# Cross-attention on one core: score tiles from products of 234, 234 and 156 columns in place of 308 and twice 154

## The chip, the core and the metric

The kernel runs on one NeuronCore of a Trainium2 chip. The core has five engines with a queue of instructions each: PE (TensorE, matrix products; its weight loads are listed as PEld), DVE (VectorE), ACT (ScalarE), POOL (GpSimd) and SP (SyncE, which here only issues DMAs). Each engine works through its own queue strictly in the order written; they meet through semaphores. Products go to PSUM, everything else lies in SBUF or in DRAM. The metric is the device time of one execution in microseconds (us); lower is better.

## The reference, cut to what matters

The input x holds 32 batches of 512 queries with 640 channels, and the context 32 batches of 77 keys with 1024 channels. Text, object, other and IP keys are named in the reference, but with 77 context rows only the text part has any keys, so this is left:

```python
q = heads(x @ to_q_w)                      # 20 heads of 32 channels
k, v = heads(ctx @ to_k_w), heads(ctx @ to_v_w)
s = einsum('bhqd,bhkd->bhqk', q, k) / sqrt(32)
p = softmax(s, axis=-1)                    # over 77 keys
out = merge(einsum('bhqk,bhkd->bhqd', p, v)) @ to_out_w + to_out_b + x
```

All of it is float32. The kernel reaches that with products of a faster format (fp32r) by splitting each operand a into a high part (the rounded value) and a low part (the rest), and adding three products: high by high, low by high, high by low.

## The kernel before, in words

A *chunk* is 128 channels of one batch, which is four heads of 32; a batch has five chunks and the kernel 160. Keys and values of all batches are made at the start and stored in DRAM (`k_dram`, `v_dram`). Then a loop runs over the batches. For each chunk it does the following, with the names of the functions and tiles:

- `queries` (L542): 15 products of 512 columns put the chunk's queries into the PSUM tile `pq`. ACT writes their high part to `qt[:, 0]` (`high_query`, L779). POOL copies halves of it to other rows (`copy_query`, L783), and DVE writes the low parts beside them (`low_query`, L787, two instructions). Tile `qt` has three planes of 128 rows: plane 0 the high queries of all four heads; plane 1 the low queries of heads 0 and 1 in rows 0 to 63 and a copy of their high queries in rows 64 to 127; plane 2 the same for heads 2 and 3.
- `score_tile` (L577): for each of four groups of 128 queries, three products into one PSUM tile `sc` of four heads by 77 keys: plane 0 by the high keys of all heads (308 columns), plane 1 and plane 2 by high and low keys of two heads each (154 columns). The weights of these products, which PE must load first, are 128 by 128 pieces of `qt`; the moving operand is the key tile `kb`.
- `load_head_keys` (L512): the key tiles `kb` (`kb0` for chunks 0 to 2 of a batch, `kb1` for chunks 3 and 4) are refilled for every batch by DMAs from `k_dram` on SP's queue, two for each of four heads and each of the two tiles: 16 in a batch. The high keys are needed twice, and the second copy is made by POOL (`copy_half_keys`, L519, four in a batch).
- `score_max` (L588, DVE), `exps` (L602, ACT: four exponentials with their sums), `sums` (L612, DVE), `normalize` (L617, POOL, over the whole chunk's `pn`), `block_transpose` (L624, DVE), then out to DRAM and back in another layout (`store_p` L633, `load_rows` L648 and L650).
- `cast_rows` (L661, L663, ACT), `rest_p` (L672, DVE) and `last_p` (L679, POOL) split the probabilities into high and low parts `pp`; `value_pass` (L694) makes six products of 512 columns from them, into `pa`.
- `lower_half`, `add_halves`, `high_a`, `low_a` (L708, L712, L726, L731) sum and split the result, and `project` (L750) multiplies by `to_out_w`: 24 products of 320 columns to a chunk. The residual and the bias come in through `xr` (`add_bias`, L743, POOL; `add_output`, L765, DVE).
- The next batch's x is transposed by DVE (L306) and split by ACT (L316) and POOL (`low_x`, L320).

The order of all this is written out by hand in three lists of tokens: FILL for batches 0 and 1 and the start, PLAN for each of the batches 2 to 30, LAST for the rest. A token such as `3k0` is an operation (`k`: one `copy_query`) of the chunk 3 places on from the batch's first; `s` is a score tile, `l` is `last_p`, `R` is `rest_p`, `N` the normalization, `uk` a load of keys. `run` walks a list and each token appends its instructions to the queues of its engines. So each engine's order is that of its tokens in the list.

Of the kernel before, what the change touches and what calls it, by code (L numbers as in the profile page):

```python
# [8 lines left out]
F32 = mybir.dt.float32  # L9
FPR = mybir.dt.float32r  # L10
AF = mybir.ActivationFunctionType
ALU = mybir.AluOpType
# [19 lines left out]
NBLK = HPC * KPAD // Q  # L32

# [18 lines left out]
def kernel(  # L52
# [394 lines left out]
    def open_small():  # L447
        nonlocal small
        if small is None:
            kvc.release()  # L450
            xpool.append(ctx.enter_context(tc.tile_pool(name="xparts", bufs=1, reuse_waits="tile")))
            small = ctx.enter_context(tc.tile_pool(name="small", bufs=1, reuse_waits="tile"))
            kbs.append(small.tile([P, 4, GROUPS[0][1], KCOLS // 2], FPR, name="kb0"))
# [9 lines left out]
    def open_second():  # L463
        nonlocal z
        if not vbs:
# [3 lines left out]
            kbs.append(pool.tile([P, 4, GROUPS[1][1], KCOLS // 2], FPR, name="kb1"))  # L469
# [33 lines left out]
    def load_keys(b, g, heads=range(HPC), parts=(0, 1)):  # L503
        j0, nj = GROUPS[g]
        src = k_dram[g][:, :, :, b * NKEY : (b + 1) * NKEY].bitcast(F32)
        kb = kbs[g].bitcast(F32)
        for i in heads:
            own, half = slice(i * HD, (i + 1) * HD), slice(i % 2 * NKEY, (i % 2 + 1) * NKEY)
            other = slice(*((i + 2) % HPC * HD + k for k in (0, HD)))
            for part, rows in enumerate((own, other)):  # L510
                if part in parts:
                    nc.sync.dma_start(kb[rows, 1 + i // 2, :, half], src[own, part])  # L512

    def load_head_keys(b, g, i, part):
        load_keys(b, g, (i,), (part,))

    def copy_half_keys(g, h):
        kb, rows = kbs[g], slice(64 * h, 64 * h + 64)
        nc.gpsimd.tensor_copy(kb[rows, 3 * h], kb[rows, 1 + h].bitcast(F32))  # L519

    def copy_keys(g):
        copy_half_keys(g, 0)
        copy_half_keys(g, 1)
# [26 lines left out]
    def split_q(n):  # L550

        qt, pq = qts[n % 2], pqs.pop(n)
        nc.scalar.copy(qt[:, 0, :], pq)
        lower, upper = slice(0, 64), slice(64, P)
        halves = ((lower, upper), (upper, lower))
        for w, (r, other) in enumerate(halves):
            nc.gpsimd.tensor_copy(qt[other, 1 + w, :], qt[r, 0, :].bitcast(F32))
        for w, (r, other) in enumerate(halves):
            nc.vector.tensor_tensor(
                qt[r, 1 + w, :], pq[r], qt[r, 0, :].bitcast(F32), ALU.subtract  # L560
            )

    def score_tile(n, t):
        b, j = divmod(n, NC_)
        g = GROUP_OF[j]
        qt, kb = qts[n % 2], kbs[g]
        jg = j - GROUPS[g][0]
        sc = ps.tile([P, S], F32, tag="sc", name="sc", bufs=3)
        half = KCOLS // 2
        for m, (cols, keys_) in enumerate(  # L570
            (
                (slice(0, KCOLS), kb[:, 0::3, jg]),
                (slice(0, half), kb[:, 1, jg]),
                (slice(half, KCOLS), kb[:, 2, jg]),
            )
        ):
            nc.tensor.matmul(  # L577
                sc[:, cols],
                qt[:, m, t * P : (t + 1) * P],
                keys_,  # L580
                start=(m == 0),
                stop=(m == 2),
            )
        return sc

    def score_max(sc):
        nm = small.tile([P, HPC], F32, tag="nm", name="nm", bufs=3)
        nc.vector.tensor_reduce(  # L588
            nm, sc[:, :KCOLS].rearrange("p (h k) -> p h k", k=NKEY), AX.X, ALU.max, negate=True
        )  # L590
        return nm

    def scores(n, t):
        sc = score_tile(n, t)
        return sc, score_max(sc)

    def exps(n, t, sc, nm):
        if n not in sms:
            sms[n] = small.tile([P, NQ * HPC], F32, tag="sm", name="sm", bufs=2)
        for i in range(HPC):  # L600
            at = t * HPC + i
            nc.scalar.activation(  # L602
                pnb[n % 2][:, at, :NKEY],
                sc[:, i * NKEY : (i + 1) * NKEY],
# [176 lines left out]
    def copy_query(n, w):  # L781
        qt, half = qts[n % 2], (slice(0, 64), slice(64, P))
        nc.gpsimd.tensor_copy(qt[half[1 - w], 1 + w, :], qt[half[w], 0, :].bitcast(F32))  # L783

    def low_query(n, w):
# [342 lines left out]
```

## Time and profile before

| | |
|---|---|
| time, median of 3 runs | 1860.13 us (1859.85 to 1861.66) |
| span of the profiled execution, first to last instruction | 1856.5 us |
| time of the runs that lies around that span (the profiled execution's own time is not given apart) | 3.4 to 5.2 us, 3.6 at the median |
| granted PE clock | 1.000 |
| matrix products | 10332 |
| POOL instructions | 1120 |
| DMA: mean rate over the span | 232 GB/s |
| HBM read and written | 247 MB and 182 MB |

A busy share adds the recorded times of an engine's instructions. Products are recorded longer than the distance at which they follow each other, so a PE of 99% busy may still wait a little. The program has a start of some 250 us (keys and values), a filling stretch of two batches, and then repeats itself from batch to batch until close to the end; a batch has 5 x (15 + 12 + 6 + 24) = 285 products.

### The profile page before, as it was taken

What the parts mean: (1) busy time and instruction counts of PE and PEld (TensorE: products, weight loads), DVE (VectorE), ACT (ScalarE), POOL (GpSimd) and SP (SyncE); (2) the same over time, 40 slices, a digit from 0 to 9 for tenths busy, and PEclk for the clock granted to TensorE, in tenths of its full rate; (3) what the DMA queues carried; (4) which work ended last, traced back from release to release, by engine and by line L of the source; (5) the groups of instructions that cost most, each with busy time, mean ns of one, the idle gap of its engine ahead of it and who ended that gap; (6) DMA issues with size and microseconds to landing.
All of it is one profiled execution on the core that took longest, in us unless ns stands there. A gap on an engine that the chain in (4) does not pass through costs nothing.

```text
span 1856.5 us, 37492 instructions
## 1 busy us (share of the span) xinstructions
PE 1842.4 (99%) x10332; PEld 1655.7 (89%) x10332; DVE 1563.4 (84%) x2502; ACT 1527.2 (82%) x6218; POOL 1303.9 (70%) x1120
## 2 busy tenths in 40 slices
PE   9999999999999999999999999999999999999998
PEld 7888897889999999999999999999999999999998
DVE  5445458899999999999999999999999999999996
ACT  3233248899999999999999999999999999999984
POOL 1100268778788788778778877887778878877874
PEclk9999999999999999999999999999999999999999
DMA  9889779998998898888998888998889988888875
GB/s 188 199 198 249 184 193 256 254 242 235 247 240 243 240 238 232 242 235 236 238 244 237 234 243 237 244 238 237 235 234 244 244 241 236 237 232 243 228 228 187
DMA packets 563296, 431.37 MB, mean 232 GB/s; under 512 B 191120, under 2 KB 471120, under 8 KB 563088
## 3 DMA queue, kind: packets, MB, share of 16 engines
q1 hardware_dynamic: 558192, 413.16, 84.5%
q0 software_dynamic: 4800, 15.65, 2.7%
q8 instruction: 85, 1.39, 0.3%
q14 instruction: 123, 1.01, 0.2%
q10 hardware_dynamic: 96, 0.16, 0.0%
HBM read 247.17 MB, written 181.64 MB: 231 GB/s over the span
## 4 chain that ended last, share of the span: by engine, by line
PE 93%; DMA 4%; SPq 1%; DVE 1%; ACT 1%; issue 0%; POOL 0%; DVEq 0%; ACTq 0%; POOLq 0%
PE po L750 29%; PE pq L542 28%; PE pa L694 12%; PE sc L577 11%; PE pv L204 7%; PE pk L204 6%; DMA pd<-z 1%; DMA cs<-in_ctx_dram 1%; DMA xr<-in_x_dram 1%; DMA wo_s<-wo_dram 0%; DMA wraw<-in_L_xattn_to_v_w_dram 0%; DMA xs<-in_x_dram 0%; DMA wraw<-in_L_xattn_to_k_w_dram 0%; ACT pn L602 0%; DMA raw<-pd 0%
## 5 line engine op out<-in xcount | busy, mean ns | idle before, releaser
L602 ACT ACTIVATE pn<-sc,nm 128x77 f32<-128x77 f32 x2560 | 797.1, 343 | 36.0 <-DVE nm L588 29.6
L750 PE MATMUL po<-wo_s,at 128*128 128x320 f32 x3840 | 707.2, 310 | 0.1
L750 PEld LDWEIGHTS po<-wo_s,at 128*128 128x128 f32 x3840 | 619.7, 188 | 41.1 <-DVE xr L765 0.6
L542 PE MATMUL pq<-xt,wq_s 128*128 128x512 f32 x2400 | 596.7, 394 | 2.9 <-ACT pp L661 1.9
L602 ACT ACTIVATION_READ_ACCUMULATOR pn<-sc,nm 128x1 f32 x2560 | 567.5, 222 | 0.0
L542 PEld LDWEIGHTS pq<-xt,wq_s 128*128 128x128 f32 x2400 | 436.7, 188 | 82.5 <-ACT pp L661 2.1
L617 POOL TENSOR_TENSOR pn<-pn,rs 128x1232 f32<-128x1232 f32 x160 | 389.4, 2434 | 94.0 <-DVE rs L612 90.0
L694 PE MATMUL pa<-pp,vb 128*128 128x512 f32 x960 | 340.9, 403 | 4.1 <-DVE at L731 3.3
L577 PEld LDWEIGHTS sc<-kb,qt 128*128 128x128 f32 x1920 | 302.9, 188 | 14.4 <-ACT pn L602 1.8
L588 DVE TENSOR_REDUCE nm<-sc 128x4 f32<-128x308 f32 x640 | 295.0, 466 | 21.6 <-PE sc L577 16.7
L577 PE MATMUL sc<-kb,qt 128*128 128x154 f32 (+1 forms) x1920 | 301.9, 274 | 0.9 <-ACT pn L602 0.9
L783 POOL CAST qt<-qt 64x512 fp32r<-64x512 f32 x320 | 196.9, 615 | 139.5 <-ACT qt L779 124.4
L712 DVE TENSOR_TENSOR pa<-pa,aw 64x512 f32<-64x512 f32 x320 | 222.3, 695 | 50.4 <-ACT aw L708 43.2
L679 POOL TENSOR_TENSOR pp<-raw,pp 64x512 fp32r<-64x512 f32 x160 | 207.0, 1294 | 66.9 <-ACT pp L661 53.5
L624 DVE STREAM_TRANSPOSE z<-pn 128x1280 f32<-128x1280 f32 x160 | 241.2, 1507 | 8.8 <-DMA pd<-z 3.4
L708 ACT COPY aw<-pa 64x1024 f32<-64x1024 f32 x160 | 162.2, 1014 | 85.0 <-PE pa L694 83.9
L787 DVE TENSOR_TENSOR qt<-pq,qt 64x512 fp32r<-64x512 f32 x320 | 216.8, 678 | 13.9 <-ACT qt L779 9.0
L320 POOL TENSOR_TENSOR xt<-xs,xt 128x512 fp32r<-128x512 f32 x160 | 204.6, 1305 | 20.8 <-ACT xt L316 15.8
L743 POOL TENSOR_TENSOR xr<-xr,bias 128x640 f32<-128x640 f32 x128 | 202.3, 1581 | 13.1 <-issue 3.5
L672 DVE TENSOR_TENSOR pp<-raw,pp 128x1024 fp32r<-128x1024 f32 x160 | 195.7, 1223 | 0.0
L694 PEld LDWEIGHTS pa<-pp,vb 128*128 128x128 f32 x960 | 173.8, 189 | 15.1 <-DVE pp L672 2.3
L663 ACT CAST pp<-raw 128x1024 fp32r<-128x1024 f32 x160 | 168.1, 1051 | 0.7 <-DMA raw<-pd 0.7
(46 smaller groups left out, 1584.2 us busy)
## 6 DMA issues: line engine op xcount, KB each, us to landing
pd<-z SPq DMA_DIRECT2D x640, 160.0 KB, 3.4
raw<-pd SPq DMA_DIRECT2D x160, 512.0 KB, 4.5
xr<-in_x_dram SPq DMA_DIRECT2D x128, 320.0 KB, 3.9
out_dram<-xr SPq DMA_DIRECT2D x127, 320.0 KB, 3.7
xs<-in_x_dram SPq DMA_DIRECT2D x124, 320.0 KB, 5.8
raw<-pd SPq DMA_DIRECT2D x160, 128.0 KB, 4.2
v_dram<-vs SPq DMA_DIRECT2D x80, 192.0 KB, 4.0
k_dram<-ks POOLq DMA_DIRECT2D x20, 512.0 KB, 4.2
```

The source lines that it names most:

```text
L204: nc.tensor.matmul(held[j][:, :gn], w[:, k, a, :], cts[g, k][:, c, :gn], start=(k == 0 and n == 0), stop=(k == NK - 1 and n == 2),)
L542: nc.tensor.matmul(pqs[n], wq_s[:, k, a, j * P : (j + 1) * P], xts[b, k][:, c, :], start=(k == 0 and m == 0), stop=(k == NC_ - 1 and m == 2),)
L577: nc.tensor.matmul(sc[:, cols], qt[:, m, t * P : (t + 1) * P], keys_, start=(m == 0), stop=(m == 2),)
L588: nc.vector.tensor_reduce(nm, sc[:, :KCOLS].rearrange("p (h k) -> p h k", k=NKEY), AX.X, ALU.max, negate=True)
L602: nc.scalar.activation(pnb[n % 2][:, at, :NKEY], sc[:, i * NKEY : (i + 1) * NKEY], AF.Exp, bias=nm[:, i : i + 1], accum_out=sms[n][:, at : ...
L617: nc.gpsimd.tensor_tensor(pf, pf, rs.unsqueeze(2).to_broadcast([P, NQ * HPC, NKEY]), ALU.mult)
L624: nc.vector.transpose(z.rearrange("p b t j -> p t b j"), pn.rearrange("p (t h) k -> p t (h k)", t=NQ).rearrange("p t (b i) -> p t b i", i=Q),)
L679: nc.gpsimd.tensor_tensor(pp[64:, 4, :], raw[:64, 2, :], pp[:64, 4, :].bitcast(F32), ALU.subtract)
L694: nc.tensor.matmul(pas[n][:, p, :], vb[:, p, t, :], pp[:, c, :], start=(c == p), stop=(c == p + 2),)
L712: nc.vector.tensor_tensor(pa[64 * p : 64 * p + 64, 0], pa[:64, p], aw[:, p], ALU.add)
L750: nc.tensor.matmul(pos[b, t, h][:, :HALF], ats[b * NC_ + j][:, a, t * P : (t + 1) * P], wos[0][:, j, c, h * HALF : (h + 1) * HALF], start= ...
L787: nc.vector.tensor_tensor(qt[rows, 1 + w, :], pqs[n][rows], qt[rows, 0, :].bitcast(F32), ALU.subtract)
```

## The change

It makes the same score tile from other pieces. Three products have 3 x 4 = 12 quadrants of 32 rows to fill, and four heads have three terms each, which is 12 as well. The heads now stand in the tile in the order 2, 0, 1, 3, each in a block of 78 columns of which 77 are used. The first product covers the blocks of heads 2, 0 and 1 (234 columns), the second those of heads 0, 1 and 3 (234), the third those of heads 2 and 3 (156). `KEYS_OF` says into which product, quadrant and block each of a head's three key pieces (high, low, high again) goes; `COPIES` says which quadrants of `qt` hold copies of high queries.

```diff
+KBLK = NKEY + 1
+ORDER = (2, 0, 1, 3)
+KEYS_AT = (0, 3 * KBLK, 6 * KBLK)
+KEYS_OF = (
+    ((0, 0, 1), (0, 3, 1), (1, 0, 0)),
+    ((0, 1, 2), (1, 2, 1), (1, 1, 1)),
+    ((0, 2, 0), (2, 0, 0), (2, 2, 0)),
+    ((1, 3, 2), (2, 1, 1), (2, 3, 1)),
+)
+COPIES = ((2, 0, 64, 64), (1, 96, 96, 32), (1, 64, 32, 32), (0, 96, 0, 32))
...
-    def copy_half_keys(g, h):
-        kb, rows = kbs[g], slice(64 * h, 64 * h + 64)
-        nc.gpsimd.tensor_copy(kb[rows, 3 * h], kb[rows, 1 + h].bitcast(F32))
...
     def load_head_keys(b, g, i, part):
-        load_keys(b, g, (i,), (part,))
+        src = k_dram[g][i * HD : (i + 1) * HD, part % 2, :, b * NKEY : (b + 1) * NKEY].bitcast(F32)
+        m, quad, block = KEYS_OF[i][part]
+        c0 = KEYS_AT[m] + block * KBLK
+        nc.sync.dma_start(
+            kbs[g].bitcast(F32)[quad * HD : (quad + 1) * HD, :, c0 : c0 + NKEY], src
+        )
...
+        for m, heads in enumerate((blocks[:, 0:3], blocks[:, 1:4], blocks[:, 0::3])):
+            nh = (3, 3, 2)[m]
+            keys_ = kb[:, KEYS_AT[m] : KEYS_AT[m] + nh * KBLK].rearrange("p (h k) -> p h k", k=KBLK)
             nc.tensor.matmul(
-                sc[:, cols],
+                heads,
                 qt[:, m, t * P : (t + 1) * P],
                 keys_,
                 start=(m == 0),
                 stop=(m == 2),
+                skip_group_check=True,
             )
...
-        for i in range(HPC):
-            at = t * HPC + i
+        for i, head in enumerate(ORDER):
+            at = t * HPC + head
...
     def copy_query(n, w):
-        qt, half = qts[n % 2], (slice(0, 64), slice(64, P))
-        nc.gpsimd.tensor_copy(qt[half[1 - w], 1 + w, :], qt[half[w], 0, :].bitcast(F32))
+        qt, (m, r1, r0, rn) = qts[n % 2], COPIES[w]
+        nc.gpsimd.tensor_copy(qt[r1 : r1 + rn, m, :], qt[r0 : r0 + rn, 0, :].bitcast(F32))
```

So a chunk now has four `copy_query` instead of two: one of 64 rows and three of 32. The last of them puts the high queries of head 0 over those of head 3 in plane 0, so it must come after the copies that read head 3 there and after the second `low_query`. The four `copy_half_keys` of a batch are gone, and the second high keys come by DMA: 24 key loads in a batch instead of 16. FILL and LAST keep their order but for the new tokens; PLAN is a new list. Line numbers after L500 are smaller by up to 27 in the new kernel (L783 is L759, L617 is L593, L577 is L558).

On POOL's queue, a stretch of about a batch in the repeating part (`qt` are the query copies, `kb` the key copies, `pn` the normalization, `pp` is `last_p`, `xt` is `low_x`, `xr` the bias). Before:

```order
L679 TENSOR_TENSOR pp<-raw,pp 64x512
L617 TENSOR_TENSOR pn_1922<-pn_1922,rs 128x16x77
L783 CAST qt_1920<-qt_1920 64x512 x2
L519 CAST kb_2003<-kb_2003 64x308 x2
L743 TENSOR_TENSOR xr<-xr,bias 128x640
L617 TENSOR_TENSOR pn_1921<-pn_1921,rs 128x16x77
L783 CAST qt_1919<-qt_1919 64x512 x2
L679 TENSOR_TENSOR pp<-raw,pp 64x512
```

And now:

```order
L655 TENSOR_TENSOR pp<-raw,pp 64x512
L593 TENSOR_TENSOR pn_1924<-pn_1924,rs 128x16x77
L759 CAST qt_1922<-qt_1922 32x512
L759 CAST qt_1922<-qt_1922 64x512
L330 TENSOR_TENSOR xt<-xs,xt 128x512
L759 CAST qt_1922<-qt_1922 32x512 x2
L330 TENSOR_TENSOR xt<-xs,xt 128x512 x2
L655 TENSOR_TENSOR pp<-raw,pp 64x512
```

The key copies have gone, each pair of query copies has become four, and they now stand in two groups with other work between them.

On PE's queue, around a score tile (`sc`) with products of `po` (projection) and `pa` (values) beside it. Before:

```order
L577 MATMUL sc<-kb_1753,qt_1919 128x308
L577 MATMUL sc<-kb_1753,qt_1919 128x154 x2
L694 MATMUL pa<-pp,vb_2005 128x512
L750 MATMUL po<-wo_s,at_2690 128x320 x3
L577 MATMUL sc<-kb_1753,qt_1919 128x308
L577 MATMUL sc<-kb_1753,qt_1919 128x154 x2
```

And now:

```order
L558 MATMUL sc<-kb_2007,qt_1923 128x234 x2
L558 MATMUL sc<-kb_2007,qt_1923 128x2x78
L670 MATMUL pa<-pp,vb_2010 128x512 x3
L726 MATMUL po<-wo_s,at_2714 128x320 x6
L558 MATMUL sc<-kb_2007,qt_1923 128x234 x2
L558 MATMUL sc<-kb_2007,qt_1923 128x2x78
```

The tile is still three products, of 624 columns in all instead of 616, and the other products stand around it in another order.

On SP's queue, where the last keys of the next batch's first tile (`kb_1753`) are called for, with the returns of probabilities (`raw`) and x (`xs`) near them. Before:

```order
L512 DMA kb_1753<-k_dram_60 32x3x77
L648 DMA raw<-pd 128x2x512
L633 DMA pd<-z 32x10x128
L512 DMA kb_1753<-k_dram_60 32x3x77
L633 DMA pd<-z 32x10x128 x3
```

And now:

```order
L517 DMA kb_1753<-k_dram_60 32x3x77 x2
L626 DMA raw<-pd 64x512
L517 DMA kb_1753<-k_dram_60 32x3x77
L312 DMA xs<-in_x_dram 32x16x160 x2
L626 DMA raw<-pd 64x512
L517 DMA kb_1753<-k_dram_60 32x3x77
```

There are twelve of these loads where eight stood. In the list the last of them now comes behind the third score tile of the batch's last chunk; before, it came just ahead of that chunk's first.

More of the change, by code (lines that the diff above doesn't have):

```diff
@@ L452, in open_small @@
             small = ctx.enter_context(tc.tile_pool(name="small", bufs=1, reuse_waits="tile"))
-            kbs.append(small.tile([P, 4, GROUPS[0][1], KCOLS // 2], FPR, name="kb0"))
+            kbs.append(small.tile([P, GROUPS[0][1], 8 * KBLK], FPR, name="kb0"))
     def open_first():
@@ L468, in open_second @@
             pool = ctx.enter_context(tc.tile_pool(name="second", bufs=1, reuse_waits="tile"))
-            kbs.append(pool.tile([P, 4, GROUPS[1][1], KCOLS // 2], FPR, name="kb1"))
+            kbs.append(pool.tile([P, GROUPS[1][1], 8 * KBLK], FPR, name="kb1"))
             z = pool.tile([P, NBLK, NQ, Q], F32, name="z")
@@ L501, in open_late @@
             wos.append(late[0].tile([P, NC_, 2, C], FPR, name="wo_s"))
[L503 to L512, printed above, removed]
-    def load_head_keys(b, g, i, part):
-        load_keys(b, g, (i,), (part,))
-    def copy_half_keys(g, h):
-        kb, rows = kbs[g], slice(64 * h, 64 * h + 64)
[L519 to L523, printed above, removed]
+    def load_head_keys(b, g, i, part):
+        src = k_dram[g][i * HD : (i + 1) * HD, part % 2, :, b * NKEY : (b + 1) * NKEY].bitcast(F32)
[4 more added lines that the diff above has]
+        )
     def load_values(b, g, segments=SEGMENTS):
@@ L548, in queries, with score_blocks @@
                 )
[L550 to L561, printed above, removed]
+    def score_blocks(sc):
+        return sc[:, : HPC * KBLK].rearrange("p (h k) -> p h k", k=KBLK)
     def score_tile(n, t):
@@ L565, in score_tile @@
         g = GROUP_OF[j]
-        qt, kb = qts[n % 2], kbs[g]
-        jg = j - GROUPS[g][0]
+        qt, kb = qts[n % 2], kbs[g][:, j - GROUPS[g][0]]
         sc = ps.tile([P, S], F32, tag="sc", name="sc", bufs=3)
[L569 to L576, printed above, removed]
+        blocks = score_blocks(sc)
+        for m, heads in enumerate((blocks[:, 0:3], blocks[:, 1:4], blocks[:, 0::3])):
+            nh = (3, 3, 2)[m]
+            keys_ = kb[:, KEYS_AT[m] : KEYS_AT[m] + nh * KBLK].rearrange("p (h k) -> p h k", k=KBLK)
             nc.tensor.matmul(
-                sc[:, cols],
+                heads,
                 qt[:, m, t * P : (t + 1) * P],
@@ L587, in score_max @@
         nm = small.tile([P, HPC], F32, tag="nm", name="nm", bufs=3)
-        nc.vector.tensor_reduce(
-            nm, sc[:, :KCOLS].rearrange("p (h k) -> p h k", k=NKEY), AX.X, ALU.max, negate=True
-        )
-        return nm
-    def scores(n, t):
-        sc = score_tile(n, t)
-        return sc, score_max(sc)
+        nc.vector.tensor_reduce(nm, score_blocks(sc)[:, :, :NKEY], AX.X, ALU.max, negate=True)
+        return nm
     def exps(n, t, sc, nm):
@@ L949, in issue @@
             low_x(b + 1, arg[0])
-        elif op == "K":
-            copy_half_keys(*arg)
         elif kind == "r":
```

2 lines of the change are left out of this document (1 added, 1 removed), and 169 rows, old and new, of tables (FILL, LAST_, PLAN).

## The prediction, made before the changed kernel was run

> **What bounds the kernel now.** I read the page's totals first, then the sums over the repeating part (600 to 1800 us), then PE's and POOL's order of time inside one batch.
>
> ```profile
> PE 1842.4 (99%) x10332; PEld 1655.7 (89%) x10332; DVE 1563.4 (84%) x2502; ACT 1527.2 (82%) x6218; POOL 1303.9 (70%) x1120
> PE 93%; DMA 4%; SPq 1%; DVE 1%; ACT 1%; issue 0%; POOL 0%; DVEq 0%; ACTq 0%; POOLq 0%
> 600.00:1800.00 1200.00, 1200.00 (x6982) 1092.39 (x6982) 1099.42 (x1763) 1108.87 (x4644) 962.31 (x809) 1.00 0.89 238
> ```
>
> The first row is the page's busy time, the second its chain of work that ended last, the third one stretch with PE, PEld, DVE, ACT and POOL in turn, then clock, DMA share and GB/s. The chain is PE. In the stretch PE is busy all the time; 6982 products at 285 a batch are 24.5 batches, so a batch takes 49.0 us. DVE and ACT stand at 92%, POOL at 80%. PE is the bound, but the other engines are not far off, and which of them has room is what this change is about.
>
> **What a score tile costs PE.** PE's order of time, then that of its weight loads (start, length, what):
>
> ```profile
> 1001.47 0.49 PE L577 MATMUL sc<-kb,qt 128*128 128x308 f32 x3
> 1001.79 0.43 PE L694 MATMUL pa<-pp,vb 128*128 128x512 f32 x1
> 1002.06 0.60 PE L750 MATMUL po<-wo_s,at 128*128 128x320 f32 x3
> 1002.49 0.40 PE L694 MATMUL pa<-pp,vb 128*128 128x512 f32 x1
> 1002.73 0.49 PE L577 MATMUL sc<-kb,qt 128*128 128x308 f32 x3
> 1003.05 0.44 PE L694 MATMUL pa<-pp,vb 128*128 128x512 f32 x1
> 1003.33 0.60 PE L750 MATMUL po<-wo_s,at 128*128 128x320 f32 x3
> 1003.77 0.39 PE L694 MATMUL pa<-pp,vb 128*128 128x512 f32 x1
> 1004.00 0.31 PE L750 MATMUL po<-wo_s,at 128*128 128x320 f32 x1
> ...
> 1002.98 0.19 PEld L694 LDWEIGHTS pa<-pp,vb 128*128 128x128 f32 x1
> 1003.09 0.43 PEld L750 LDWEIGHTS po<-wo_s,at 128*128 128x128 f32 x2
> ```
>
> Starts count here, not lengths. Three products of 320 columns pass in 0.44 us (1003.33 to 1003.77), 0.147 each or 0.46 ns a column. A 512-column `pa` behind `po` takes 0.24 (1002.49 to 1002.73). From a score tile's start to the product behind its `pa` it is 0.59 and 0.60 (1001.47 to 1002.06, 1002.73 to 1003.33), so the tile costs about 0.36. By columns it would be 616 x 0.46 ns = 0.28. The rest is weight loads: two of them follow at 0.11 us (1002.98, 1003.09), and a product of 154 columns (0.07) can't hide the next load. So now 0.14 + 0.11 + 0.11 = 0.36.
>
> The new tile has 234, 234 and 156 columns, 0.108, 0.108 and 0.072 by the same rate, each beside a load of 0.11: 0.33. That is 0.03 less for each of a batch's 20 tiles, 0.6 us. If nothing else held it, PE would go at 49.0 - 0.6 = 48.4 us a batch, and 32 batches would save 19 us. The strided output of the third product I price at nothing: the first product's strided operand costs nothing visible today. Reduction and exponentials keep their 77 columns a head. Also nothing.
>
> **What POOL gets.** POOL's rows of one batch, from one normalization to the same one of the next (in brackets its idle time and what ended it):
>
> ```profile
> 999.86 2.28 POOL L617 TENSOR_TENSOR pn<-pn,rs 128x1232 f32<-128x1232 f32 x1 [1.65 <-DVE rs L612]
> 1002.20 1.28 POOL L783 CAST qt<-qt 64x512 fp32r<-64x512 f32 x2
> 1003.55 0.94 POOL L519 CAST kb<-kb 64x308 fp32r<-64x308 f32 x2
> 1004.57 1.57 POOL L743 TENSOR_TENSOR xr<-xr,bias 128x640 f32<-128x640 f32 x1
> ...
> 1011.02 1.28 POOL L783 CAST qt<-qt 64x512 fp32r<-64x512 f32 x2 [2.64 <-ACT qt L779]
> ...
> 1021.60 1.26 POOL L783 CAST qt<-qt 64x512 fp32r<-64x512 f32 x2 [1.28 <-ACT qt L779]
> ...
> 1029.88 3.06 POOL L617 TENSOR_TENSOR pn<-pn,rs 128x1232 f32<-128x1232 f32 x1 [0.50 <-DVE rs L612]
> ...
> 1035.21 1.20 POOL L519 CAST kb<-kb 64x462 fp32r<-64x462 f32 x2
> 1036.48 0.61 POOL L783 CAST qt<-qt 64x512 fp32r<-64x512 f32 x1
> 1038.22 1.29 POOL L679 TENSOR_TENSOR pp<-raw,pp 64x512 fp32r<-64x512 f32 x1 [1.13 <-ACT pp L661]
> 1040.03 2.27 POOL L617 TENSOR_TENSOR pn<-pn,rs 128x1232 f32<-128x1232 f32 x1 [0.52 <-DVE rs L612]
> ...
> 1045.89 1.30 POOL L679 TENSOR_TENSOR pp<-raw,pp 64x512 fp32r<-64x512 f32 x1 [0.60 <-ACT pp L661]
> 1048.85 2.27 POOL L617 TENSOR_TENSOR pn<-pn,rs 128x1232 f32<-128x1232 f32 x1 [1.65 <-DVE rs L612]
> ```
>
> The batch is 48.99 us, and the bracketed waits after the first row add up to 8.32. So POOL works 40.67, with the small gaps between its instructions. The four key copies go: 1.02 (1003.55 to 1004.57) and 1.27 (1035.21 to 1036.48), -2.29. Ten query copies come. A pair takes 1.35 (1002.20 to 1003.55), 0.67 each. No row shows a 32-row copy; whether rows matter at all is told by these two groups:
>
> ```profile
> L679 POOL TENSOR_TENSOR pp<-raw,pp 64x512 fp32r<-64x512 f32 x160 | 207.0, 1294 | 66.9 <-ACT pp L661 53.5
> L320 POOL TENSOR_TENSOR xt<-xs,xt 128x512 fp32r<-128x512 f32 x160 | 204.6, 1305 | 20.8 <-ACT xt L316 15.8
> ```
>
> The same operation takes 1294 ns on 64 rows and 1305 on 128. I take 0.67 for 32 rows; the bounds are 0.34 (half, if rows counted) and 0.67. So +6.7, and by the lower bound of the 15 narrow ones +1.7. POOL's work becomes 45.1 us, which a batch of 48.4 would still hold.
>
> **What POOL can't do at the same time.** One DVE instruction, `rest_p` (L672), reads two operands from SBUF. Here it is beside POOL, and the usual length of it and of the normalization:
>
> ```profile
> 1029.65 1.16 DVE L672 TENSOR_TENSOR pp<-raw,pp 128x1024 fp32r<-128x1024 f32 x1
> ...
> 349.61 1.29 POOL L679 TENSOR_TENSOR pp<-raw,pp 64x512 fp32r<-64x512 f32 x1 [1.02 <-ACT pp L661]
> 349.76 2.22 DVE L672 TENSOR_TENSOR pp<-raw,pp 128x1024 fp32r<-128x1024 f32 x1
> ...
> L672 DVE TENSOR_TENSOR pp<-raw,pp x160: 1159/1208/2224, 289.9 to 1838.7; 128x1024 fp32r<-128x1024 f32 x160
> L617 POOL TENSOR_TENSOR pn<-pn,rs x160: 2265/2281/3137, 264.7 to 1821.0; 128x1232 f32<-128x1232 f32 x160
> ```
>
> The normalization that began 0.23 after `rest_p` (1029.88 against 1029.65) took 3.06 instead of 2.28: POOL stood still until 1.01 us after `rest_p` began. And the `rest_p` that began while POOL was at `last_p` (349.76) took 2.22 instead of 1.21. So the two exclude each other, whoever is first. In the batch above four of the five `rest_p` fall mostly into POOL's waits and only one costs it anything (0.78). With the new load they don't fit there any more: 48.4 - 45.1 leaves 3.3 us of waits for four times 1.2.
>
> The sum for a POOL that is always busy: 45.1, less the 0.78 that is a block already, plus five blocks of 1.01, less a gap of 0.06 that each block may cover (the pair's 1.35 is two lengths of 0.615, which leaves 0.06 a copy): 45.1 - 0.8 + 5.0 - 0.3 = 49.1. That is over PE's 48.4 and 0.1 above the whole batch of today. On top come waits that remain. POOL's order is fixed, and a normalization can't start before its reciprocal, which hangs on exponentials of scores that waited for POOL's copies. The nearest rows are those waits of today, 0.50 and 0.52; I take one of them a batch, 0.5. The bounds are none and all the waits on reciprocals and casts that no `rest_p` fills, 0.50 + 0.52 + 0.60 = 1.6. So a batch takes 49.6 (49.1 to 50.7), 0.6 over today.
>
> [...]
>
> **The other parts.** The fourth copy now waits for the second `low_query`, and on POOL's queue `low_x`, `last_p` and the normalization stand behind it; score tiles, queries of the next batch and value products wait for these. No stall is added as long as POOL is late anyway, since it finds its inputs ready; that is why I add no separate term. DVE waits for POOL inside `rest_p` by up to a normalization; at 92% now it has 4 us a batch free. DMA: these two groups are the key loads in the stretch.
>
> ```profile
> kb<-k_dram SPq DMA_DIRECT2D x192, 28.9 KB, 2.9
> kb<-k_dram SPq DMA_DIRECT2D x199, 19.2 KB, 3.2
> ```
>
> Four more of each a batch are 192 KB, at 238 GB/s 0.8 us of the engines, which have 11% of 49 us free. The last load of the first tile's keys stands ahead of 15 query products (3.5 us at 0.23) and two projection steps (0.9) before the tile that needs it; it lands in 2.9. Cost nothing, with 1.5 us to spare; if a late wait on SP's queue eats that, the tile is late by the rest. Against that, the copy that sat between the loads and the tile is gone.
>
> **Start and end.** FILL and LAST hold three batches of the 32.
>
> ```profile
> 300.00:348.50 48.50, 43.36 (x223) 35.90 (x222) 42.13 (x69) 44.03 (x189) 40.85 (x38) 1.00 0.93 266
> ```
>
> In the filling stretch POOL is busy 40.85 of 48.5 already and PE waits 5 us, so the 4.4 us that POOL gains meets little room. I price these batches like the others. Sum: 32 x (49.6 - 49.0) = +20, on a span of 1856.5 gives 1876, and with the 3.6 us around it 1880.
>
> **Rivals.**
> 1. *POOL is the bound, with few waits* (above): 49.1 (no wait) to 50.1 (two of 0.5) a batch, 1863 to 1895. Chance 0.50.
> 2. *The engines' waits chain.* DVE and ACT stand at 92%; a `rest_p` that waits out a normalization (2.28) delays reductions behind it, these the exponentials, these the next normalization. With all three waits of today kept the batch is 50.7 and the time 1860 + 32 x 1.7 = 1915; more is possible. For it: three engines near the top with fixed queues. Against it: in the list, waits for query copies are one to three us apart from the tiles that use them. Chance 0.23.
> 3. *Narrow copies are cheap, PE stays the bound (the other side).* It decides when a copy of 32 rows costs under 0.6 or so of one of 64: then POOL with blocks comes to 49.1 - 15 x 0.27 = 45, and PE goes at 48.4. Time 1860 - 19 = 1841. Against it: 1294 against 1305 ns. [...] Today's pairs write different halves and still follow at 0.67, with 0.61 of work; for 32 rows no run here shows it. Chance 0.20.
> 4. *It cancels, or the narrower products don't save what they should:* POOL's blocks partly hidden, 49.0 a batch, 1860. Chance 0.07.
>
> **How the numbers follow.** The forecast is the first: 1880. Less than 0.2% (3.7 us) is about what a measurement can't tell from no change. Faster is rival 3, 0.20; same is rival 4, 0.07; slower the first two, 0.73. The range goes from rival 3's 1841 to a little over rival 2's 1915, 1840 to 1922: it leaves out half of rival 3 below and a tail of rival 2 above. The forecast's own range is 1863 to 1895.
>
> **What the profile will show.** Right: POOL busy over 90% in the repeating part, waits of POOL on `qt` and `rs` mostly gone, `rest_p` or POOL's instructions lengthened many times, PE idle before score tiles with POOL as releaser, 32-row copies of about 615 ns, a score tile of 0.33 on PE. Wrong: copies of 32 rows much shorter or overlapping, PE without waits at 48.4 a batch; or, if PE waits for DMA or DVE instead, another bound than I argue.

## The result, and the profile after

The changed kernel takes 2029.47 us (2026.76 to 2038.03, 4 runs) beside 1859.99 us for the kernel before on the same chip: a ratio of 1.092 (95% interval 1.090 to 1.095). It is slower, as forecast, but by 170 us and not by 20, and outside the range.

The page's busy times of the changed kernel, and then the same repeating part (columns PE, PEld, DVE, ACT, POOL, clock, DMA share, GB/s):

```profile
PE 1889.4 (93%) x10332; PEld 1665.6 (82%) x10332; DVE 1604.9 (79%) x2502; ACT 1543.1 (76%) x6218; POOL 1504.4 (74%) x1312
```

```profile
600.00:1800.00 1200.00, 1119.07 (x6336) 995.05 (x6335) 1028.89 (x1601) 1018.90 (x4222) 1014.41 (x864) 0.98 0.81 219
```

6336 products are 22.2 batches, so a batch takes 54.0 us instead of 49.0. No engine is full any more: PE is busy 93% of the stretch, POOL 85%, DVE and ACT less than before, and the DMA engines move 219 GB/s instead of 238. Where nothing is full, something is late. By the 3000th product the kernel is 44 us behind the one before (637.4 against 593.6 us after the span's start), and the 24 batches of the next 6840 products lose another 124 (54.2 against 49.0 each).

The waits of that stretch (total us, times, longest us), those of PE, ACT and DVE that matter here:

```profile
ACT at L702 <- DVE pa L688: 94.3, 47, 4.0
...
DVE z L600 <- DMA pd<-z: 84.0, 47, 4.1
...
PE sc L558 <- DMA kb<-k_dram: 27.0, 18, 3.1
...
PE sc L558 <- DMA raw<-pd: 24.9, 12, 3.0
...
PE pa L670 <- ACT pp L639: 15.2, 14, 2.2
```

PE waits for loads: for keys, and, through the cast `pp` that needs them, for probabilities (`raw`). The row in which `sc` waits for `raw` belongs to the keys too. A score product reads no probabilities, and in the trace PE's queue gets past its semaphores each of those 12 times 0.03 or 0.04 us after the last piece of a key load has landed. The profile names another load, whose semaphore is asked for as well. So 51.9 us of the stretch are waits for keys. For query copies of POOL it waits 1.5 us in 1200 (3 times). DVE's transposes (`z`) wait for the stores of the last `z`. Of the last four rows the kernel before has none. On SP's own queue, first in the kernel before and then in the changed one:

```profile
SPq L648 <- DMA pd<-z: 27.1, 47, 1.8
```

```profile
SPq L626 <- DMA pd<-z: 88.0, 87, 3.8
SPq L715 <- DMA out_dram<-xr: 45.0, 46, 1.4
```

SP waits three times as long for a store of probabilities to land before it may call them back, and everything behind waits with it. One such place, SP's order of time (start, length, what) and PE's:

```profile
1043.73 2.45 SPq L517 DMA_DIRECT2D kb<-k_dram  x4
1046.54 0.45 SPq L626 DMA_DIRECT2D raw<-pd  x1
1047.04 1.05 SPq L517 DMA_DIRECT2D kb<-k_dram  x2
```

```profile
1046.34 0.38 PE L558 MATMUL sc<-kb,qt 128*128 128x234 f32 x2
1049.12 0.92 PE L558 MATMUL sc<-kb,qt 128*128 128x156 f32 x4 [2.40 <-DMA raw<-pd]
```

SP issues from 1043.73 to 1046.18 without a longer break. The `raw` load at 1046.54 could go only when its store had landed (1046.47), which holds the queue for another 0.36 us. The key load behind it goes at 1047.04, its last piece lands at 1049.04, and PE stands still until then before the third product of a score tile. That product needs low and second high keys. More follows behind the stop (last columns: clock, DMA share, GB/s):

```profile
1049.50:1050.50 1.00, 1.00 (x5) 0.90 (x5) 1.00 (x5) 0.85 (x2) 0.00 (x0) 0.50 0.99 351
...
1051.50:1052.50 1.00, 1.00 (x4) 0.71 (x4) 1.00 (x1) 0.72 (x2) 1.00 (x1) 0.50 0.94 298
1052.50:1053.50 1.00, 1.00 (x6) 0.95 (x5) 1.00 (x1) 0.78 (x2) 0.54 (x2) 0.85 1.10 421
```

For three microseconds PE is granted half its clock, and six products of 512 columns take 2.64 us (1049.84 to 1052.48), where six took 1.40 before the stop (1043.81 to 1045.21).

### The profile page after: what moved, and what is told of

The parts are those of the page before. It is cut to its first block, busy times and chain, and to the rows that moved or that the text cites. A ratio compares the mean times of both kernels' runs of the same rounds, so it can differ in the third digit from the quotient of the medians.

```text
span 2025.0 us, 38116 instructions
## 1 busy us (share of the span) xinstructions
PE 1889.4 (93%) x10332; PEld 1665.6 (82%) x10332; DVE 1604.9 (79%) x2502; ACT 1543.1 (76%) x6218; POOL 1504.4 (74%) x1312
## 5 line engine op out<-in xcount | busy, mean ns | idle before, releaser
L538 PE MATMUL pq<-xt,wq_s 128*128 128x512 f32 x2400 | 666.3, 406 | 2.8 <-DVE qt L763 1.4
L578 ACT ACTIVATION_READ_ACCUMULATOR pn<-sc,nm 128x1 f32 x2560 | 554.2, 217 | 0.0
L759 POOL CAST qt<-qt 32x512 fp32r<-32x512 f32 (+1 forms) x640 | 423.9, 662 | 76.0 <-ACT qt L755 33.2
L593 POOL TENSOR_TENSOR pn<-pn,rs 128x1232 f32<-128x1232 f32 x160 | 366.2, 2289 | 135.5 <-DVE rs L588 123.6
L558 PEld LDWEIGHTS sc<-kb,qt 128*128 128x128 f32 x1920 | 298.3, 191 | 123.7 <-DMA raw<-pd 34.8
L558 PE MATMUL sc<-kb,qt 128*128 128x234 f32 (+1 forms) x1920 | 301.0, 268 | 84.9 <-DMA kb<-k_dram 38.2
L670 PE MATMUL pa<-pp,vb 128*128 128x512 f32 x960 | 310.9, 411 | 40.9 <-ACT pp L639 19.7
L655 POOL TENSOR_TENSOR pp<-raw,pp 64x512 fp32r<-64x512 f32 x160 | 250.5, 1565 | 26.3 <-ACT pp L637 6.9
L719 POOL TENSOR_TENSOR xr<-xr,bias 128x640 f32<-128x640 f32 x128 | 217.6, 1701 | 53.5 <-DMA xr<-in_x_dram 38.2
L648 DVE TENSOR_TENSOR pp<-raw,pp 128x1024 fp32r<-128x1024 f32 x160 | 244.1, 1525 | 12.2 <-ACT pp L639 12.1
L330 POOL TENSOR_TENSOR xt<-xs,xt 128x512 fp32r<-128x512 f32 x160 | 204.7, 1295 | 23.4 <-ACT xt L326 16.1
L702 ACT CAST at<-pa 128x512 fp32r<-128x512 f32 x160 | 94.7, 592 | 128.9 <-DVE pa L688 128.8
```

What stands on the lines that cost most here:

```text
L538: nc.tensor.matmul(pqs[n], wq_s[:, k, a, j * P : (j + 1) * P], xts[b, k][:, c, :], start=(k == 0 and m == 0), stop=(k == NC_ - 1 and m == 2),)
L558: nc.tensor.matmul(heads, qt[:, m, t * P : (t + 1) * P], keys_, start=(m == 0), stop=(m == 2), skip_group_check=True,)
L578: nc.scalar.activation(pnb[n % 2][:, at, :NKEY], sc[:, i * KBLK : i * KBLK + NKEY], AF.Exp, bias=nm[:, i : i + 1], accum_out=sms[n][:, at ...
L593: nc.gpsimd.tensor_tensor(pf, pf, rs.unsqueeze(2).to_broadcast([P, NQ * HPC, NKEY]), ALU.mult)
L648: nc.vector.tensor_tensor(pp[:, 2:4, :], raw[:, 0:2, :], pp[:, 0:2, :].bitcast(F32), ALU.subtract)
L655: nc.gpsimd.tensor_tensor(pp[64:, 4, :], raw[:64, 2, :], pp[:64, 4, :].bitcast(F32), ALU.subtract)
```

## Experiments

Each time stands beside the kernel before on the same chip (1859.2 to 1860.0 us). "Two wide copies" means that the three copies of 32 rows are left out and a 64-row copy of plane 1 stands in for two of them, so some rows of two query planes don't hold the head that they should; the work elsewhere is the whole.

### First four: the list, the tile, the copies, one load

The first theory was that the new PLAN is at fault, with its late loads, and that with the old list the rest costs little. Rivals: POOL, as the prediction had it, or the new tile. The first kernel keeps tile, four copies and 24 key loads and takes the old PLAN, with the new tokens beside those they belong to:

```diff
-0ux3 0r 0k0 0uk120 0uk111 1d1 1d0 0v1 0v0 0s2 0g1 0N 0p16 0m1
...
+1uv10 0r 0e0 0s2 0ux3 0g0 0N 0v0 1uv15 0v1 0m1 0v2 0f10 0p16
...
+0uk120 0uk122
...
+0k0 0k1
...
```

> The new tile, the new copies and the 24 key loads, with the old kernel's list for the repeating part: each old query copy becomes two of the new ones at its place, each new key load stands beside the old one of its head, the key copies are left out. Theory A, POOL and rest_p exclude each other and POOL is the bound (the prediction): the order doesn't matter much, 49.1 to 50.1 us a batch, 1863 to 1895. Theory B, the new list calls for keys and probabilities too late on SP's queue, whose issues take 0.43 us each: the old list has 5 us of lead for the keys, so PE is the bound again, 48.4 to 48.7 us a batch, 1841 to 1852. Theory C, the narrower products themselves are slow on PE: over 1900.

Measured 1960.59 us, ratio 1.0535 (1.0517 to 1.0552). The batch is an even 52.2 us. PE's waits in the stretch:

```profile
PE sc L558 <- POOL qt L759: 40.2, 47, 1.1
PE pa L670 <- POOL pp L655: 16.0, 46, 1.0
```

Nearly all of them are POOL's: here the prediction's mechanism stands, and larger than priced. So the new list is 69 us of the 170, and the old list is far from curing the rest.

The second moves one key load, the one of the stop above, four microseconds ahead:

```diff
-2T3 2p37 0uk131 2l
+2T3 2p37 0uk121 0uk131 2l
...
-3q1 3d1 0uk121 2p34
+3q1 3d1 2p34
```

> The changed kernel with one token moved: the last load of the second key tile (head 2, low) stands ahead of the load of head 3 some 4 us earlier, in place of two steps ahead of the first score tile that needs it. Theory A: within 10 us of the changed kernel's 2029. Theory B: the wait of 2.6 us before that tile goes, and with it the stretch of some 3 us at half the PE clock behind it, which cost some 1 us; 1.5 to 3.5 us a batch less, 1915 to 1980.

2036.18 us, 1.0948: no gain. PE's waits for keys fall from 51.9 to 9.7 us, but those behind ACT's `pp` rise from 15.2 to 24.9 and those behind `rest_p` from 7.1 to 20.4, and 21.3 us for `xr` are new. In all PE waits 87.1 us of the stretch where it waited 80.5. The stop that one sees is not the cause: others grow in its place.

The third has the new list, 24 loads and no POOL key copies, but the old tile and two 64-row copies; the fourth is the changed kernel with two wide copies. Their edits, in this order:

```diff
-        c0 = KEYS_AT[m] + block * KBLK
...
+        row = i * HD if part != 1 else (i + 2) % HPC * HD
+        plane = 3 * (i // 2) if part == 2 else 1 + i // 2
+        nc.sync.dma_start(kb[row : row + HD, plane, :, half], src)
...
+                (slice(0, KCOLS), kb[:, 0::3, jg]),
+                (slice(0, half), kb[:, 1, jg]),
+                (slice(half, KCOLS), kb[:, 2, jg]),
```

```diff
+        if w > 1:
+            return
-        qt, (m, r1, r0, rn) = qts[n % 2], COPIES[w]
+        qt, (m, r1, r0, rn) = qts[n % 2], ((2, 0, 64, 64), (1, 64, 64, 64))[w]
```

> The changed kernel's order and its 24 key loads, but the old tile of 308 and twice 154 columns and two query copies of 64 rows (in place of the first and the last of the four). Theory A: POOL is freed of ten copies a batch, 49.0 to 49.5 us a batch, 1860 to 1875. Theory B: the order and SP's queue hold it, 2000 to 2045. Theory C: 1860.

> The changed kernel with two query copies of 64 rows in place of the four, at the places of the first two; the third and fourth are left out, so the terms of heads 0 and 1 that need them are not computed. Theory A: 48.4 to 49.0 us a batch, 1841 to 1862. Theory B: POOL has 4.4 us a batch less to do but was not the bound, 1990 to 2030.

1997.75 us (1.0741) and 2038.71 (1.0962). Taking two copies a chunk off POOL gains nothing in the new list, so POOL's work is not what holds it there. The old tile with two copies is 41 us better than the new one with two, but still 138 above the kernel before. Why the two tiles differ here was not taken apart; with 16 loads and the old list, below, the new one is no slower.

### SP's queue

What the four have in common is 24 key loads. The next four runs ask for that. The first is the old list with the new tile, but two wide copies:

```diff
+        if w not in (0, 2):
+            return
-        qt, (m, r1, r0, rn) = qts[n % 2], COPIES[w]
+        qt, (m, r1, r0, rn) = qts[n % 2], ((2, 0, 64, 64), (1, 64, 64, 64))[w // 2]
```

> The old list with the new tile as before, but two query copies of 64 rows in place of the four, so terms of some heads are not computed; all key loads and the narrower products stay. Theory A1 (with the old list POOL and its block by rest_p are the bound): PE is the bound again and shows what the narrower products save, 48.4 to 48.7 us a batch, 1841 to 1852. Theory B1 (with the old list the eight more key loads on SP's queue hold it): 1900 to 1960.

1954.74 us, 1.0509: hardly less than with four copies. POOL's bound is gone, another stands right behind it. Its waits:

```profile
DVE z L600 <- DMA pd<-z: 42.7, 46, 2.4
...
ACT pp L639 <- DMA raw<-pd: 41.0, 20, 3.9
...
PE pa L670 <- DVE at L707: 21.1, 21, 2.1
...
ACT pp L637 <- DMA raw<-pd: 17.5, 18, 2.4
```

Probabilities come late, ACT stands at their cast by up to 3.9 us, and DVE and PE behind it. The second run is the changed kernel with six loads moved on SP: four loads of probabilities that stood close behind the stores they wait for (`1d1`, `1d0`, `2d1`, `5d1`), one load of the residual (`3ur1`), and the key load of the second run above (`0uk121`, not printed again). The third leaves out the third key load of each head from the third batch on (those rows keep old keys):

```diff
-0uk111 1d1 1d0 0v1
+0p19 1d1 1d0 1uv16
...
-0p22 2d1 1v4
+1z 2d1 1ur0
...
-3X2 3ur1 3p0
+4q1 3ur1 2uv06
...
-4p10 5d1 4p9
+4e1 5d1 5d0
```

```diff
+        if part == 2 and b > 1:
+            return
```

> The changed kernel with six loads moved on SP's queue and nothing else: four loads of probabilities that stood 1 to 2 us behind the stores they read now stand 4 us or more behind them, the last load of the second key tile stands 4 us earlier, one residual load some 5 us later. Theory B2 (in the new list SP's queue stands still behind loads whose stores have not landed, and what is behind comes late): SP's wait for the stores falls from 4 us a batch to under 1.5 and the batch from 54.2 to 50 to 52.5, 1890 to 1970; then POOL shows. Theory D (the loads are late because z is late, whatever SP does): 2000 to 2030.

> The changed kernel without the third of the three key loads of each head from the third batch on, so its high keys stay those of an earlier batch: eight issues of 0.44 us a batch less on SP's queue, 3.5 us. Theory B3 (SP's time for issues is the bound): 3 to 4 us a batch less, 1905 to 1935. Theory B2 (order and waits, not the number of issues): 0 to 1.5 us a batch less, 1980 to 2030.

1980.67 us (1.0641) and 1979.38 (1.0640). Each gives 49 to 50 us: the same loads in a better order, or fewer loads. SP's waits for the stores of probabilities, in the same order:

```profile
SPq L626 <- DMA pd<-z: 0.7, 2, 0.4
```

```profile
SPq L628 <- DMA pd<-z: 99.4, 108, 4.0
```

They were 88.0 us in the changed kernel. So the first of the two runs takes away waits and leaves all the issues, and the second takes away issues and leaves the waits. Both count.

The last is the cleanest: the kernel before, with its tile, its two copies and its list, in which only the second high keys come by DMA and POOL's key copies are gone:

```diff
-            for part, rows in enumerate((own, other)):
...
-                    nc.sync.dma_start(kb[rows, 1 + i // 2, :, half], src[own, part])
...
+        row = i * HD if part != 1 else (i + 2) % HPC * HD
+        plane = 3 * (i // 2) if part == 2 else 1 + i // 2
+        nc.sync.dma_start(kb[row : row + HD, plane, :, half], src)
```

> Before's tile, copies and list, but the second high keys come by DMA (24 loads a batch, beside the old ones) and POOL's key copies are gone. Theory A1: PE stays the bound, 49.0 us a batch, 1857 to 1863. Theory B1: the eight more loads cost on SP's queue, 1880 to 1960.

1930.73 us, 1.0389 (1.0359 to 1.0418). Eight more loads a batch on SP's queue, with less work on POOL, cost 71 us.

### Is it the loads, or what they carry?

The eight loads are more issues on SP, but also 192 KB more a batch. To part these, the keys are kept in DRAM as high, high and low, so that one load of one head fills both of its high places: the bytes into `kb` stay, the issues are 16 again. The price is a second store of each high key piece at the start. First with the old tile, then with the new one and two wide copies (its blocks are laid out so that a head's two places are neighbours):

```diff
-    k_dram = [dram.tile([P, 2, nj, NT], FPR, name=f"k_dram{j0}") for j0, nj in GROUPS]
+    k_dram = [dram.tile([P, 3, nj, NT], FPR, name=f"k_dram{j0}") for j0, nj in GROUPS]
...
+        engine.dma_start(dst[:, 1:3], ks[:, :, :gn])
+        engine.dma_start(dst[:, 0], ks[:, 0, :gn])
...
+        if part == 0:
+            nc.sync.dma_start(
+                kb[i * HD : (i + 1) * HD, 2 * (i // 2) : 2 * (i // 2) + 2, :, half], src[:, 0:2]
+            )
```

> The kernel before's list, tile and two query copies; the second high keys come by DMA as in the run with 24 key loads (1930.7 us), but the keys are kept in DRAM as high, high and low, so that one load of one head brings both high copies: 16 key loads a batch again, with the same bytes into SBUF, and no key copies on POOL. Theory S (the eight more issues on SP's queue, 0.44 us each, are what cost 71 us): 1855 to 1868 us, since TensorE bounds it again. Rival T (the transfers themselves cost it: more bytes and packets on the 16 DMA engines, landing late): 1900 to 1935 us.

> The new tile with the old list and two 64-row query copies in place of four (rows 0 to 31 and 96 to 127 of two query slots are not filled as the reference needs; its time with 24 key loads was 1954.7 us), now with the merged loads, 16 a batch. Theory S (SP's issues held that kernel): the tile's saving on TensorE shows at last, 48.4 us a batch in place of 49.0, so 1840 to 1852 us. Theory S in part (the tile has a cost of its own that no run has shown): 1860 to 1900 us. Rival T (transfers): 1930 to 1960 us.

1874.04 us, 1.0076 (1.0061 to 1.0091), and 1863.33, 1.0015 (1.0005 to 1.0025): 57 and 91 us less than the same kernels with 24 loads. The stretch of the old tile with 24 loads, with 16, and of the new tile with 16:

```profile
600.00:1800.00 1200.00, 1174.34 (x6727) 1052.32 (x6726) 1056.21 (x1698) 1071.95 (x4486) 884.99 (x686) 1.00 0.87 234
```

```profile
600.00:1800.00 1200.00, 1200.00 (x6979) 1092.16 (x6978) 1099.35 (x1764) 1109.11 (x4650) 912.46 (x711) 1.00 0.91 242
```

```profile
600.00:1800.00 1200.00, 1198.14 (x7027) 1085.62 (x7026) 1101.57 (x1775) 1116.40 (x4677) 921.65 (x716) 1.00 0.93 244
```

That is 50.8, 49.0 and 48.7 us a batch. With 16 loads more bytes move in the same time, at a DMA share of 0.91 and 0.93, and it does no harm. The DMA packets of a batch are as many with the old tile and 24 loads as with 16 (16.3 and 16.1 thousand). SP's issues are what differs: with the old tile they add up to 946 us of the stretch for 24 loads and to 861 for 16 (868 in the kernel before), 1935 and 1807 of them. So the transfers are not the cause, the issues on SP's queue are. The waits of ACT for `raw` (58.5 us in the two rows of the kernel with 24 loads and two copies) are nearly gone with 16:

```profile
ACT pp L642 <- DMA raw<-pd: 2.3, 3, 1.7
...
ACT pp L644 <- DMA raw<-pd: 1.0, 3, 0.5
```

What is left of the first kernel's loss, 14 us, lies ahead of the repeating part: it reaches its 3000th product at 610.6 us, against 593.6, most of it lost where the start now stores each high key piece twice. And the new tile's gain on PE can be seen at last: 0.3 us a batch.

### POOL alone

With 16 loads the whole change under the old list shows POOL's part by itself:

> The whole change (new tile, four query copies) with the old list, its output complete, and merged loads, 16 a batch in place of 24 (with 24: 1960.6 us). The prediction's POOL term is alone here: theory P (POOL, with 45 us of work and the DVE operations that exclude it, bounds the batch at 49.6 to 50.7 us): 1878 to 1920 us. Rival S alone (POOL has room once SP has): 1840 to 1856 us. Rival T: 1940 to 1965 us.

1960.45 us, 1.0546: the same as with 24 loads (1960.59). So SP's lateness costs nothing where POOL is later still: two bounds of almost the same height, and taking away either one alone shows the other. POOL's costliest groups in the stretch:

```profile
L598 POOL TENSOR_TENSOR pn<-pn,rs 128x1232 f32<-128x1232 f32 x116 | 264.3, 2278 | 46.5 <-DVE rs L593 44.6
L764 POOL CAST qt<-qt 32x512 fp32r<-32x512 f32 x345 | 211.2, 612 | 20.7
L660 POOL TENSOR_TENSOR pp<-raw,pp 64x512 fp32r<-64x512 f32 x116 | 169.5, 1461 | 36.0 <-issue 28.6
...
L764 POOL CAST qt<-qt 64x512 fp32r<-64x512 f32 x115 | 80.9, 704 | 73.0 <-ACT qt L760 68.6
```

A copy of 32 rows takes 612 ns, as one of 64 does in the kernel before (615). POOL is busy 1014.6 of 1200 us, 43.9 us of each 52.0. The other 8 are small gaps and waits, above all for reciprocals (`rs`, 44.6 us of the stretch) and for ACT's cast of the queries (68.6). Two runs ask whether this is the amount of POOL's work, or that PE must wait for four copies in a row. One lets ACT make the copy that stays on its rows, straight from the product; the other has two wide copies and two useless ones into a spare buffer behind them, so that POOL works as much but PE waits for two only:

```diff
         nc.scalar.copy(qts[n % 2][:, 0, :], pqs[n])
+        nc.scalar.copy(qts[n % 2][96:P, 1, :], pqs[n][96:P])
...
+        if w == 1:
+            return
```

```diff
+            nc.gpsimd.tensor_copy(qt[r1 : r1 + 64, m, :], qt[r0 : r0 + 64, 0, :].bitcast(F32))
+        if w in (2, 3):
...
+            nc.gpsimd.tensor_copy(spare[0][96:P], qt[0:32, 0, :].bitcast(F32))
```

> The whole change with the old list and merged loads (1960.5 us), with one of the four query copies, the 32 rows that stay on their partitions, made by ScalarE straight from the product instead of by POOL; the output is complete. Theory P (POOL's work, and the wait for it, holds that kernel at 52.0 us a batch): five copies of 0.67 us go, 3.3 us a batch, and TensorE's 48.7 us bound it again, 1860 to 1880 us, if ScalarE's five more copies of some 0.6 us (45.5 + 3.0 of 48.7 us) find room. Rival A (ScalarE has no room for them): 1890 to 1960 us. Rival N (POOL does not hold it): 1950 us or more.

> The new tile with the old list, merged loads and two 64-row copies (1863.3 us), and on POOL two more copies of 32 rows for each chunk, into a spare buffer that nobody reads, both behind the second wide copy: POOL does as much work as with four copies, but TensorE waits for two. (Some rows of two query slots are not filled as the reference needs.) Theory W (the amount of POOL's work, as the prediction had it): as with four copies, 1930 to 1965 us. Rival Q (the latency of four copies in a row between the query product and its score tile): 1860 to 1890 us. In between: both.

1925.80 us (1.0359) and 1926.29 (1.0358), 50.7 and 50.8 us a batch. Both lie in between. The first takes one copy of 0.67 us a chunk off POOL, which was priced at 3.3 us a batch, and gains 1.3. PE goes on waiting for copies:

```profile
PE sc L563 <- POOL qt L767: 30.2, 48, 1.1
```

ACT is busy 1147.4 of 1200 us there, so a lack of room on ACT may be part of it; no run parts the two. The second says more. Two copies that nobody waits for cost 63 of the 97 us between two copies and four (1863.33 to 1960.45): that is POOL's amount of work. The other 34 are, by difference, the waiting for the copies themselves. PE's waits with the useless copies:

```profile
PE pa L675 <- POOL pp L660: 13.1, 47, 0.9
PE pq L542 <- POOL xt L330: 8.5, 35, 0.3
```

None is for a copy now: `last_p` and `low_x`, which stand behind the copies on POOL's queue, come late instead.

### Both cures in the new list

The changed kernel's own list, with merged loads and with the six loads moved:

> The whole change with its own new list, but merged key loads (16 a batch) and the five loads that stood close behind their stores moved on SP, both cures at once (either alone: 1979 and 1981 us, neither: 2029). Theory L (what the new list costs beside the old one is late loads on SP's queue, and behind them stands the same POOL bound as in the old list, 1960 us): 1925 to 1965 us. Rival O (the new list has a second fault, in the order of the engines' own work): 1970 us or more.

1922.98 us, 1.0338 (1.0322 to 1.0353), 106 us less than the changed kernel and 37 less than the old list with four copies. So the new list is not bad in itself: it is better for the four copies (POOL is busy 1097 of 1200 us, where it was 1015 under the old list), and lost that and more by late loads.

```profile
600.00:1800.00 1200.00, 1166.59 (x6746) 1044.00 (x6745) 1123.12 (x1704) 1085.54 (x4503) 1097.48 (x924) 1.00 0.88 235
```

```profile
L764 POOL CAST qt<-qt 32x512 fp32r<-32x512 f32 x356 | 258.4, 726 | 26.9 <-ACT qt L760 5.0
L660 POOL TENSOR_TENSOR pp<-raw,pp 64x512 fp32r<-64x512 f32 x119 | 181.7, 1527 | 9.4
```

Part of that busy time is not work: a narrow copy takes 726 ns here and not 612, and `last_p` 1527 and not 1294, while `rest_p` takes 1802 ns on average where it took 1337 under the old list. By these lengths POOL and `rest_p` hold each other up more.

Of the 64 us that it still lies above the kernel before, some 26 are lost by the 3000th product (619.2 us against 593.6); the rest is 50.7 us a batch. No version here beats the kernel before.

## Why the prediction was wrong

**The other parts: the failed step.** The prediction priced eight more loads by their bytes (0.8 us of the DMA engines) and by the landing of one load of the first key tile: "Cost nothing, with 1.5 us to spare". The bytes do cost nothing. The time of SP was not priced. Added up over the stretch of the kernel before, SP's issues take 868 of 1200 us, 35 of the 49 us of a batch (1812 of them, 0.44 us each in the median), on one queue that also stands at loads whose store hasn't landed (27.1 us in 47 waits). Eight more are 3.5 us. Alone they cost 1.8 us a batch (71 us in all), in the old list with the new tile 3.0. In the new list, where loads stand closer behind their stores, leaving them out gives 1.6 a batch (50 us), and merging them with the six loads moved 3.3: that is 106 of the 170 us. The sentence that "a late wait on SP's queue" might eat the 1.5 us named the right event, but gave it no chance and no price; and the second key tile, whose load PE then stood for, wasn't looked at. The prediction's last sign of being wrong, that PE waits for DMA, is what the profile shows.

**What POOL can't do at the same time.** This was right in kind and wrong in its place. A copy of 32 rows costs 0.61 (forecast: 0.67 with its gap). In the changed kernel POOL hardly makes PE wait, since PE and POOL are late already. So it is in part luck that the time moved the way that was forecast.

With cured loads POOL bounds the batch at 52.0 us in the old list, against a forecast of 49.6 (49.1 to 50.7). There the term for `rest_p` was too large and that for waits too small. With four copies `last_p` takes 1461 ns instead of 1294 and the wide copy 704 instead of 615, which is 5 x 0.17 + 5 x 0.09 = 1.3 us a batch and not five blocks of 1.01. The waits that remain are 6 us (141.8 of the stretch, 28.6 of them without a releaser that the profile shows) and not 0.5. "POOL that is always busy" was the false premise: its queue is fixed, and it stood for reciprocals and casts even when it was the bound.

In the new list, for which the sum was made, the sum comes closer. The instructions are longer by 15 x 0.114 for the narrow copies, 5 x 0.164 for the wide ones and 5 x 0.233 for `last_p`, 3.7 us a batch where 5.0 was forecast. The waits are 2.0 (48.0 of the stretch) where it was 0.5. The batch takes 50.7, the upper bound. But PE waits less for query copies there (13.2 us of the stretch) than for `rest_p` and `low_a` of DVE (11.2 and 7.5), so POOL is not the only bound. The second rival's 1915 us is near that run's 1923; its mechanism, waits that chain through POOL, DVE and ACT, fits these rows, but not the changed kernel.

**What a score tile costs PE.** The saving is about right. Over the stretch a tile was 0.149 + 0.072 + 0.111 = 0.33 us before (means from start to start), not 0.36, and is 0.116 + 0.114 + 0.079 = 0.31 with merged loads and two copies: 0.023 less a tile, 0.5 us a batch, where 0.6 was forecast; 0.3 arrived. In no other run could it be seen.

**Start and end.** These were priced like the other batches. By the 3000th product the changed kernel is 44 us late, and even with 16 loads and two copies 17. The list for the start, FILL, was not taken apart further.

**Rivals.** Cheap narrow copies fell (612 ns). The one that decided was not among them: loads that come late on SP's queue.

## What to carry to other kernels

A queue that only issues DMAs has a load like an engine has (here 868 of 1200 us in issues before the change): count its issues, their time and its blocking waits per loop, before adding a transfer whose bytes are small. Merging two loads into one can be worth more than moving a copy off an engine (57 and 91 us here, against 35). And where taking one suspect away changes nothing, take away two together: here POOL and SP stood within 6 us of each other under the old list, and each hid the other.

## What was unexpected of the hardware

Half a clock after a short stop. In the changed kernel's stretch PE has 31 gaps of over 1.3 us from one product to the next (0.15 is the median). Behind none of the 12 up to 2.02 us does the granted clock fall; behind 13 of the 19 from 2.13 to 3.38 us it is 0.50 to 0.74 in the window from 0.8 to 2.3 us after the stop. What parts those 13 from the other six isn't shown. The mean of 0.98 over the stretch is some 24 us of the 1200 at full clock.

How far `rest_p` and POOL delay each other differs from place to place. In one place of the run with useless copies each is delayed by less than a whole instruction. DVE's and POOL's order of time there:

```profile
1004.81 1.83 DVE L653 TENSOR_TENSOR pp<-raw,pp 128x1024 fp32r<-128x1024 f32 x1
```

```profile
1004.26 1.30 POOL L330 TENSOR_TENSOR xt<-xs,xt 128x512 fp32r<-128x512 f32 x1
1006.02 1.76 POOL L769 CAST qt<-qt 64x512 fp32r<-64x512 f32 x2 [0.46 <-ACT qt L760]
```

`rest_p` (1.21 us in the median of the kernel before) overlaps `low_x` until 1005.56 and takes 1.83. The two copies then take 1.76 instead of 1.28, while `rest_p` lasts until 1006.64: about 0.5 us more. In the changed kernel the delays are longer in places: three narrow copies from 539.47 take 3.39 us, some 1.4 more than three of 0.61 with their gaps, beside a `rest_p` of 1.21 (from 541.17), and a `rest_p` that begins 0.70 after a normalization (566.20) takes 2.65.

What stays open: how the 71 us of the old list divide. With 24 loads in it SP's issues grow from 868 to 946 us of the stretch, and its waits for stores hardly change (27.1 to 32.2 us), but it also waits for older loads to land, and no run changes one of these alone there.
